# Building a four-layer network's constants earlier in the lead-in: VectorE's order of work in the first ten quarters

## The chip, the core and the metric

The kernel runs on one NeuronCore of a Trainium2 chip. The metric is the device time of one execution in microseconds (us). The profile is of one execution of the same program on the chip. The engines are TensorE (PE in the profile, PEld for its weight loads), VectorE (DVE), ScalarE (ACT), GpSimd (POOL) and the queue that issues most of the transfers (SP). Each engine takes its own instructions in program order, and semaphores tie the engines together.

## The reference, cut to what matters

The input is x of 8192 samples of 8 x 16 x 16 in float32. Four layers follow, each a residual one over a normalised input:

```
x = x + L0_conv_ref(gn(x), core0, core1, core2, bias)   # three-core tensor-train product
x = x + L1_conv_ref(gn(x), lin_w, lin_b, gamma, beta)   # 3x3 convolution, batch norm over all samples, relu
x = x + L2_conv_ref(gn(x), weight, bias)                # 3x3 convolution of quantised x and weights
x = x + L3_conv_ref(gn(x), weight, bias)                # 3x3 convolution of binarised weights, edge padding
```

`gn` is a group norm with 4 groups of 2 channels. The batch norm of layer 1 and the maximum of layer 2 need all samples, so the kernel passes over the data three times. Only the start of the first pass (layer 0 and the convolution of layer 1) matters here.

## The kernel before

**Tiles and quarters.** The samples are cut in 64 tiles of 128 samples. A tile is 128 partitions (channel and row) by 2048 elements (sample and column). Each tile is cut in four quarters of 32 samples. The first pass is the loop of lines 569 to 628 over n = 0 to 255; n is called a quarter number here, and quarter n belongs to tile t = n // 4. In quarter n, TensorE runs the second half of layer 0 for quarter n (`main`, 16 matmuls into a PSUM tile `po`), between its halves the first half of layer 0 for quarter n + 1 (`expand`, into `pu`, which ScalarE copies to `u`), and at the end, from quarter 6 on, layer 1's convolution for quarter n - 6 (`conv1`, into `pm` and `pc`). VectorE closes quarter n with `x += po` (line 414, "DVE xs<-po,xs" in the profile). The instructions of a quarter are put in order by hand: `at(r, ok, f, ...)` hangs a function on step r of the eight steps of `main`, so a lower r means an earlier place in every engine's queue.

**The norms.** Tile t + 2 is normalised for layer 0 in the quarters of tile t: its square on ScalarE (second quarter), its sums on VectorE (`norm_b_sums`, third quarter), a small chain `norm_b_stats` that ends in a power on GpSimd, and `norm_b_apply` on VectorE (fourth quarter). Tile t - 1 gets its second norm, for layer 1, in a like manner (`norm_sums`, `norm_stats`, `norm_apply`, first and second quarter). `conv1_output` on VectorE puts layer 1's output together one quarter after its matmuls.

**The halves.** From the second tile on, `expand` takes its input as two parts, a rounded high half and the rest, both read back from DRAM. `limbs(t, q)` makes them: a ScalarE copy into `xh`, a GpSimd subtraction in place ("POOL bs<-bs,xh"), and eight transfers by SP into `limb_d` ("limb_d<-xh" and "limb_d<-bs"). `fetch(t, q)` reads them back with a transfer that GpSimd issues ("xl<-limb_d"). Which quarter's halves are made where is written out in lines 614 to 617: in quarter n > 2 those of quarter n + 4, and before that by a table. GpSimd also adds layer 0's bias to each tile (`add_bias`, "POOL xs<-xs,w").

**The constants.** VectorE builds the constants of layers 1 to 3 in the lead-in, in the generator `late_constants` (lines 135 to 246). Each `next(rest, None)` at the top of a quarter issues one part, up to the next `yield`, ahead of everything else that VectorE does in that quarter. The parts are "limbs" (`core2r`), "layer 1" (group sums, `band1`, and the six combined weights `fast1`), "layer 2" (`avg16`, the quantised weights), "band 2", "layer 3" (the signs and scales), "band 3" (with `sign3`) and "statistics" (`wsum`, `quarter`, `gpad`, selectors). The condition on line 582 leaves out quarter 0 and the fourth quarter of each tile.

**Buffers.** `po`, `pm` and `pc` share three PSUM buffers in turn, so once `conv1` runs, `po` of a quarter waits for VectorE's `x += po` of the quarter before it, and `pm` and `pc` wait until `conv1_output` has read the ones before them. `pu` has one buffer, so `expand` waits for ScalarE's copy of the last one.

Of the kernel before, what the change touches and what calls it, by code (L numbers as in the profile page):

```python
# [24 lines left out]
NQ = 4  # L25
# [28 lines left out]
def tile_net(ctx: ExitStack, tc: tile.TileContext, xb, xt_in, pack0, pack1, pack2, out):  # L54
    nc = tc.nc
    NT = xt_in.shape[0]
# [33 lines left out]
    def load2(i):  # L90
        T2[i]["x"] = x_slots[i % KEEP]
        T2[i]["y"] = y_stay[i] if i < STAY else y_slots[(i - STAY + 1) % len(y_slots)]
        if i >= STAY:
            nc.sync.dma_start(T2[i]["y"], y_d[order2[i]])
            nc.sync.dma_start(T2[i]["x"], x1_d[order2[i]])
# [198 lines left out]
    with first as s:  # L294
# [19 lines left out]
        def load_b(t):  # L314
            T[t]["xb"] = bs[t % 2]
            n = F // 2 if t == 0 else F
            for a in range(0, F, n):
                nc.sync.dma_start(T[t]["xb"][:, a:a + n], xb[t][:, a:a + n])
# [84 lines left out]
        def main(t, q, between, n0=None):  # L403
            u = T[t].pop(("u", q)).rearrange("p b (s n) -> p b s n", s=R)
            po = ps_m.tile([P, BANK], F32, name=f"po_{t}_{q}", tag="mm")
            parts = [(0, QS)] if n0 is None else [(0, n0), (n0, QS)]
            for a, b in parts:
                for r in range(R):
                    for f, args in between.get(r, ()) if b == QS else ():
                        f(*args)  # L410
                    pe.matmul(samples(po)[:, a:b], core01[:, r], u[:, a:b, r, :], start=(r == 0), stop=(r == R - 1))
            cols = slice(q * BANK, (q + 1) * BANK)
            x = T[t]["x"]
            dve.tensor_tensor(x[:, cols], po, x[:, cols], ALU.add)
# [66 lines left out]
        def conv1(t, q):  # L481
            v = T[t].pop(("v", q))
            pm, po = (ps_m.tile([P, k, NC], F32, name=f"{n}_{t}_{q}", tag="mm") for n, k in (("pm", 4), ("pc", 2)))
            for ps, at in ((pm, 0), (po, 4)):
                for k in range(ps.shape[1]):
                    pe.matmul(ps[:, k], L["fast1"][:, at + k], v[:, at + k], start=True, stop=True)
            m = wk.tile([P, 2, NC], F32, name=f"m_{t}_{q}", tag="m")
            act.activation(m[:, 0], pm[:, 0], AF.Identity, bias=L["b1"], scale=1.0)
            act.copy(m[:, 1], pm[:, 2])
            T[t]["m", q] = m, pm, po  # L490
# [40 lines left out]
        def quarter_of(n, lag):  # L531

            t, q = divmod(n - lag, NQ)
            return (t, q) if 0 <= t < NT else None
# [7 lines left out]
        rest = late_constants(s.enter_context(tc.tile_pool(name="late", bufs=1)))  # L542
# [26 lines left out]
        for n in range(NT * NQ):  # L569
            t, q = divmod(n, NQ)  # L570
            steps = {}

            def at(r, ok, f, *args):
                if ok:
                    steps.setdefault(r, []).append((f, args))

            def at1(r, f, lag):
                if quarter_of(n, lag):
                    at(r, True, f, *quarter_of(n, lag))

            last, before, ahead = t == NT - 1, t > 0, t + 2 < NT
            if n > 0 and q != NQ - 1:
                next(rest, None)
            tn, qn = divmod(n + 1, NQ)
            at(0, tn < NT, expand, tn, qn, 0)
            at(4, tn < NT, expand, tn, qn, 1)
            at1(0, conv1_input, LAG)
            if n < NT * NQ - 1:
                at1(6, conv1_scaled, LAG - 1)
            if n == 0 and NT > 1:  # L590
                at(1, True, norm_b_spread, 1)
                at(1, True, norm_b_apply, 1)
                at(1, True, add_bias, 1)
            if q == 0:
                if before and t - 1 not in y_of:
                    nc.sync.dma_start(x1_d[t - 1], T[t - 1]["x"])
                at(1, before, norm_sums, t - 1)
                at(4, before, norm_stats, t - 1)
                if ahead:
                    load_b(t + 2)  # L600
            elif q == 1:
                at(1, ahead, norm_b_square, t + 2)
                at(1, before, norm_apply, t - 1)
                at(4, t + 3 < NT, load_t, t + 3)
            elif q == 2:
                at(1, ahead, norm_b_sums, t + 2)
                at(1, ahead, norm_b_stats, t + 2)
            else:
                at(1, t + 3 < NT, add_bias, t + 3)
                at(1, ahead, norm_b_spread, t + 2)  # L610
                at(1, ahead, norm_b_apply, t + 2)
            at1(3, conv1_output, LAG + 1)

            for m in {0: [], 1: [4, 5], 2: [6]}.get(n, [n + NQ]):
                at(0 if n == 1 else 2, m < NT * NQ, limbs, *divmod(m, NQ))
            for m in {0: [], 1: [4, 5], 2: []}.get(n, [n + 3]):
                at(5, m < NT * NQ, fetch, *divmod(m, NQ))
            if n == 1:
                at(5, NT > 2, add_bias, 2)
            if last:  # L620
                at(2, q > 1, quarter_apply, t, q - 2)
                at(2, q > 0, quarter_stats, t, q - 1)
            main(t, q, steps, n0=QS // 2 if n == 0 else None)
            if quarter_of(n, LAG):
                conv1(*quarter_of(n, LAG))
            if n == NT * NQ - 2 and NT > STAY + 2:
                load2(STAY)
                load2(STAY + 1)
# [435 lines left out]
```

## Time and profile before

| | |
|---|---|
| time, median of 3 | 3863.89 us (3861.8 to 3866.22) |
| span of the profiled execution | 3863.6 us |
| TensorE busy | 3612.7 us (94%) |
| VectorE busy | 3415.1 us (88%) |
| ScalarE busy | 2512.1 us (65%) |
| GpSimd busy | 3044.1 us (79%) |
| TensorE busy from 0 to 150 us | 117.14 of 150 us |
| TensorE busy from 150 to 2500 us | all but 0.04 of 2350 us |

An engine that is busy nearly all of a stretch may bound it; an idle engine with a named releaser tells what it waited for. The page's shares are averages over three passes with different limits, so a change in the lead-in is read from the timeline of the first 155 us. In a timeline line the columns are start and duration in us, engine, line, operation, output and inputs, shapes, the number of instructions merged, and in brackets the idle time before it and what ended that. Most instructions are issued through one helper and carry its line (L43), so they are told apart by the names of their tiles.

### The profile page before, as it was taken

What the parts mean: (1) busy time and instruction counts of PE and PEld (TensorE: products, weight loads), DVE (VectorE), ACT (ScalarE), POOL (GpSimd) and SP (SyncE); (2) the same over time, 40 slices, a digit from 0 to 9 for tenths busy, and PEclk for the clock granted to TensorE, in tenths of its full rate; (3) what the DMA queues carried; (4) which work ended last, traced back from release to release, by engine and by line L of the source; (5) the groups of instructions that cost most, each with busy time, mean ns of one, the idle gap of its engine ahead of it and who ended that gap; (6) DMA issues with size and microseconds to landing.
All of it is one profiled execution on the core that took longest, in us unless ns stands there. A gap on an engine that the chain in (4) does not pass through costs nothing.

```text
span 3863.6 us, 52760 instructions
## 1 busy us (share of the span) xinstructions
PE 3612.7 (94%) x16264; PEld 2130.7 (55%) x16326; DVE 3415.1 (88%) x6316; ACT 2512.1 (65%) x2673; POOL 3044.1 (79%) x3101
## 2 busy tenths in 40 slices
PE   7899999999999999999999999997665589999998
PEld 4566666666666666666666666662221145555555
DVE  7988888888888888888888888877998889999997
ACT  4566666666666666666666666665665477777775
POOL 4687777877778777777777777766887679999998
PEclk9999999999999999999999999997776699999999
DMA  5678788787887878878788788757999624444432
GB/s 210 207 253 270 253 265 266 250 269 254 264 269 249 271 252 263 269 251 268 253 264 268 253 265 255 257 185 285 423 425 425 280 92 181 185 184 183 178 153 98
DMA packets 210809, 960.93 MB, mean 249 GB/s; under 512 B 44896, under 2 KB 45152, under 8 KB 110048
## 3 DMA queue, kind: packets, MB, share of 16 engines
q1 hardware_dynamic: 173808, 692.22, 48.2%
q0 software_dynamic: 36288, 264.26, 23.2%
q8 instruction: 131, 2.15, 0.2%
q14 instruction: 150, 1.23, 0.1%
q10 hardware_dynamic: 432, 1.08, 0.1%
HBM read 578.84 MB, written 378.54 MB: 248 GB/s over the span
## 4 chain that ended last, share of the span: by engine, by line
PE 83%; DMA 6%; DVE 6%; issue 2%; POOL 1%; ACT 0%; POOLq 0%; SPq 0%; DVEq 0%; ACTq 0%
PE po L43 44%; PE pu L43 12%; PE pf L43 10%; PE pm L43 6%; PE pq L43 4%; PE s L43 3%; PE pc L43 3%; DVE top L43 2%; DMA yk<-y_d 2%; DMA x_d<-xs 1%; DMA x_d<-u 1%; DMA x_d<-xk 1%; DMA x_d<-ys 1%; DMA xk<-x_d 1%; DMA xs<-x_d 1%
## 5 line engine op out<-in xcount | busy, mean ns | idle before, releaser
L43 PE MATMUL po<-u,core 128*128 128x512 f32 (+1 forms) x4112 | 1847.0, 592 | 4.8 <-DVE xs L43 4.8
L43 ACT COPY u<-pu 128x2048 f32<-128x2048 f32 x512 | 956.4, 1868 | 527.8 <-PE pu L43 527.7
L43 PEld LDWEIGHTS po<-u,core 128*128 128x128 f32 x4112 | 745.4, 190 | 743.6 <-issue 737.5
L43 PE MATMUL pu<-core2r,xl 128*128 128x256 f32 x4032 | 679.3, 311 | 6.1 <-DMA xl<-limb_d 6.1
L43 PEld LDWEIGHTS pu<-core2r,xl 128*128 128x128 f32 x4032 | 528.8, 189 | 129.3 <-issue 128.4
L43 POOL TENSOR_TENSOR bs<-bs,xh 128x512 fp32r<-128x512 f32 (+1 forms) x253 | 324.7, 1284 | 196.0 <-ACT xh L43 196.0
L43 POOL TENSOR_TENSOR v<-e 128x128 f32<-128x128 f32 x750 | 397.4, 541 | 0.0
L43 DVE TENSOR_TENSOR xs<-po,xs 128x512 f32<-128x512 f32 x256 | 177.0, 692 | 227.1 <-PE po L43 227.1
L43 ACT ACTIVATE m<-pm,b 128x128 f32<-128x128 f32 x250 | 91.9, 368 | 405.1 <-PE pm L43 405.1
L43 PEld LDWEIGHTS pm<-v,fast 128*128 128x128 f32 x2000 | 263.7, 192 | 128.6 <-issue 109.7
L43 POOL TENSOR_TENSOR e<-x1n,x 128x512 f32<-128x512 f32 x250 | 305.9, 1224 | 23.7 <-ACT x L43 16.4
L43 DVE TENSOR_TENSOR bs<-bs,stat 128x1024 f32<-128x1024 f32 x252 | 290.8, 1216 | 2.1
L43 POOL TENSOR_TENSOR xs<-xs,w 128x2048 f32<-128x2048 f32 x64 | 291.5, 4555 | 0.5 <-DMA xs<-in_xt 0.5
L43 PE MATMUL pm<-v,fast 128*128 128x128 f32 x2000 | 265.3, 276 | 8.3 <-DVE ends L43 8.3
L43 POOL TENSOR_TENSOR mv<-mv,mhalf 128x4 f32<-128x4 f32 x127 | 130.8, 1030 | 150.3 <-DVE mv L43 150.3
L43 ACT ACTIVATE x<-x1n 128x512 f32<-128x512 f32 x500 | 246.9, 544 | 2.1 <-DVE x1n L43 2.1
L43 PE MATMUL pf<-hi,sign 128*128 128x512 f32 x768 | 226.8, 433 | 0.0
L43 POOL DMA_DIRECT2D xl<-limb_d x252 | 149.8, 594 | 97.2 <-ACT x L43 34.3
L43 PE MATMUL pf<-lo,sign 128*128 128x512 f32 x768 | 219.4, 423 | 3.4 <-ACT lo L43 3.4
L43 POOL TENSOR_TENSOR v<-r 128x128 f32<-128x128 f32 x500 | 215.5, 447 | 0.0
L43 ACT ACTIVATE sq<-xs 128x2048 f32<-128x2048 f32 (+1 forms) x107 | 199.3, 1862 | 8.0 <-POOL xs L43 4.6
L43 POOL TENSOR_TENSOR mvb<-mvb,mhalf 128x4 f32<-128x4 f32 x64 | 66.3, 1036 | 173.8 <-DVE mvb L43 173.8
(289 smaller groups left out, 7184.8 us busy)
## 6 DMA issues: line engine op xcount, KB each, us to landing
xl<-limb_d POOLq DMA_DIRECT2D x252, 1024.0 KB, 7.4
x_d<-xs SPq DMA_DIRECT2D x76, 1024.0 KB, 8.4
xs<-in_xt SPq DMA_DIRECT2D x64, 1024.0 KB, 7.5
bs<-in_xb SPq DMA_DIRECT2D x63, 1024.0 KB, 5.6
limb_d<-xh SPq DMA_DIRECT2D x1008, 64.0 KB, 4.4
limb_d<-bs SPq DMA_DIRECT2D x1008, 64.0 KB, 5.2
y_d<-ys SPq DMA_DIRECT2D x60, 1024.0 KB, 8.1
u<-x_d SPq DMA_DIRECT2D x36, 1024.0 KB, 6.1
```

What stands on the lines that cost most here:

```text
L43: return self.tc.keep_in_program_order(op(*args, **kwargs))
```

## The change

It has two parts, both in the lead-in. First, the generator is advanced in every quarter from 1 on, and twice in quarter 1. So "limbs" and "layer 1" are both built in quarter 1 (before: quarters 1 and 2), "layer 2" in quarter 2 (before 4), "band 2" in 3 (before 5), "layer 3" in 4 (before 6), "band 3" in 5 (before 8) and "statistics" in 6 (before 9). Second, the halves of quarter 7, the last of the second tile, are made in quarter 2 beside those of quarter 6, at step 0, instead of in quarter 3 at step 2; there they stood behind the third tile's `norm_b_apply` and `add_bias` in program order. Its purpose is to use VectorE's idle time in quarter 1 and to have the second tile's halves in DRAM sooner.

```diff
@@ -579,8 +579,10 @@
             last, before, ahead = t == NT - 1, t > 0, t + 2 < NT
-            if n > 0 and q != NQ - 1:
+            if n > 0:
                 next(rest, None)
+                if n == 1:
+                    next(rest, None)
             tn, qn = divmod(n + 1, NQ)
@@ -611,8 +613,8 @@
-            for m in {0: [], 1: [4, 5], 2: [6]}.get(n, [n + NQ]):
-                at(0 if n == 1 else 2, m < NT * NQ, limbs, *divmod(m, NQ))
+            for m in {0: [], 1: [4, 5], 2: [6, 7], 3: []}.get(n, [n + NQ]):
+                at(0 if n < 3 else 2, m < NT * NQ, limbs, *divmod(m, NQ))
```

## The prediction

> **What bounds the kernel now.** I began with the table of stretches, to see where TensorE is not busy.
>
> ```profile
> core 0: us, PE busy (x) PEld busy (x) DVE busy (x) ACT busy (x) POOL busy (x), PEclk, DMA share, GB/s
> 0.00:150.00 150.00, 117.14 (x495) 70.13 (x496) 127.39 (x204) 71.24 (x63) 74.21 (x86) 0.93 0.57 197
> 150.00:700.00 550.00, 550.00 (x2401) 341.18 (x2400) 487.45 (x947) 357.00 (x408) 424.78 (x583) 1.00 0.80 259
> ```
>
> From 150 us on TensorE is the bound for the rest of the first pass, at 10.08 us a quarter (the chain shows quarters ending at 154.98, 165.07, 175.14). So whatever the lead-in saves moves all that follows by the same amount, and nothing else of the change can pay. The second view is TensorE's waits from 60 to 155 us (total us, times, longest).
>
> ```profile
> PE pm L43 <- DVE ends L43: 8.3, 2, 4.2
> PE pu L43 <- DMA xl<-limb_d: 6.1, 1, 6.1
> PE po L43 <- DVE xs L43: 4.8, 2, 2.7
> ```
>
> One wait is for quarter 6's halves from DRAM, the other four for VectorE. The third view is the timeline: why is VectorE late?
>
> ```profile
> 42.08 0.69 DVE L43 TENSOR_TENSOR xs<-po,xs 128x512 f32<-128x512 f32 x1 [7.43 <-PE po L43]
> 48.57 5.07 DVE L43 TENSOR_SCALAR fast<-fast 128x128 f32<-128x128 f32 x1
> 48.95 4.59 POOL L43 TENSOR_TENSOR xs<-xs,w 128x2048 f32<-128x2048 f32 x1
> 62.01 4.55 POOL L43 TENSOR_TENSOR xs<-xs,w 128x2048 f32<-128x2048 f32 x1
> 67.74 0.62 POOL L43 DMA_DIRECT2D xl<-limb_d  x1
> 75.04 2.04 PE L43 MATMUL pu<-core2r,xl 128*128 128x256 f32 x8 [6.10 <-DMA xl<-limb_d]
> 109.59 5.13 DVE L43 TENSOR_TENSOR ys<-w,she 128x384 f32<-128x384 f32 x2
> 116.94 2.83 DVE L43 CAST sign<-band 128x384 fp32r<-128x384 f32 x1
> 130.02 5.82 DVE L43 TENSOR_SCALAR quarter<-quarter 128x4 f32<-128x4 f32 x1
> ```
>
> VectorE idles 7.43 us in quarter 1 and then is nearly gapless to 155 us. And some tiny constants take 3 to 6 us: 128x128 TENSOR_SCALARs of the same group take 0.23, and this one 5.07, ending at 53.64, just when GpSimd's `add_bias` (48.95 to 53.54) ends. Likewise `quarter`, four elements, waits from 130.02 to 135.84 while GpSimd runs without a gap to 135.81.
>
> [...]`quarter` waited out a run of nine GpSimd instructions. I use the trace: a contending instruction waits for the end of GpSimd's gapless run. [...]Here the 8 `po` matmuls after the 6.10 us wait take 4.38 us instead of 3.60, and those after a 2.71 us wait 5.12. So a removed wait also saves up to 1.5 us of slow matmuls.
>
> **The change, part by part.** The work is the same; only places move. Parts, from start to start of their neighbours: "layer 1" 42.68 to 53.83, 11.15 us, of which 4.84 is the stall shown, so 6.3 net; "layer 2" 4.4 (two short stalls of 1 us on GpSimd's subtractions; 2.4 net); "band 2" 77.34 to 80.05, 2.7; "layer 3" 86.28 to 92.93, 6.65 (4.2 stalled, 2.45 net); "band 3" 109.59 to 119.69, 10.1 (3.0 net); "statistics" 129.12 to 136.50, 7.4 (1.75 net). I place them again, taking GpSimd's and the transfers' times from the trace.
>
> *Quarter 1.* "Layer 1" starts at 34.64, when "limbs" ends. Its third tensor_tensor (36.4) meets the subtractions of 36.29 to 38.80, a stall of 2.4; it ends at 34.64 + 6.3 + 2.4 = 43.4. Behind it waits `x += po` of quarter 1, at 43.4 instead of 42.08: 1.3 us that TensorE doesn't feel, since it needs that buffer again only at 61. End 44.0.
>
> *Quarter 2.* "Layer 2" meets an idle GpSimd: 46.5. `norm_b_sums` 4.6: 51.1. The small statistics reach their tensor_scalar at 51.7, inside `add_bias` (48.95 to 53.5), behind which GpSimd now has two subtractions of 1.26 ready, quarter 6's and, moved here, quarter 7's: a run until 56.06. That is the wait the change adds, up to 4.4 us; behind it stand the power, `x += po` and all of the third tile's norm. Power 56.7 to 57.7 (before 59.76 to 60.79), `x += po` of quarter 2 by 57.3 (before 59.60). The subtractions end at 54.8 and 56.1 (before 62.0 and 67.8), so quarter 6's halves leave SP at about 55 instead of 62.07.
>
> *Quarter 3.* "Band 2" [...]stands from 57.3 against the power and the `add_bias` right behind it, 57.7 to 62.25: it can lose 4.9. Then 62.3 + 2.7 = 65.0, spread and apply 0.36 + 4.55 = 69.9, `x += po` 70.5 (before 66.4). The fetch goes out at 62.3 instead of 67.74 and, at the 7.2 us of before, lands by 69.6. But ScalarE now waits for `x += po` with its square (1.9), then the high half and the copy of `pu` (1.9 and 0.5): the one `pu` buffer is free at 74.7. So TensorE starts quarter 5 at 74.7, not 75.04: this early gain is lost again. I take this end; without the loss of 4.9 it starts at 70.
>
> *Quarters 4 and 5.* "Layer 3" 2.45: 73.0. Sums 2.3 + 2.3, statistics 1.4: 79.1 (before 76.73); quarter 7's fetch goes at 80.1 and lands at 87.7, some 2 us after TensorE wants it. `x += po` 79.7, "band 3" against a power and one subtraction, 3.0 + 1.9: 84.6; apply 5.4: 90.0; `x += po` 90.6 (before 86.3).
>
> *Quarter 6.* "Statistics" meets layer 1's input work on GpSimd (to about 92.8): 94.6. Sums 4.6, statistics 1.15, `x += po` 100.3 to 101.0 (before 98.71 to 99.4). TensorE's quarter 7 waits for that, and ends 9.35 later as before: 110.4, against 108.96. Up to here I am 1.4 us behind, but every constant is built.
>
> *Quarters 7 to 10.* No "band 3", no "statistics": 10.1 + 7.4 = 17.5 us of VectorE are gone. Quarter 8: 111.1 + 2.3 (sums) + 2.8 (conv1_output) + 3.7 (sums, statistics) = 119.9, `x += po` 120.6 (before 128.48 to 129.2). TensorE runs quarter 8 to 121.0 with no wait (its pm starts there, before 123.22), quarter 9 to 131.1 (before 139), convolution to 132.4 without the wait until 143.05, quarter 10 to 141.2. Before, this was 154.82. VectorE has 131.8 + 4.6 + 1.15 + 2.8 = 140.4 and is in time. **Gain 154.8 - 141.2 = 13.6 us**, so 3863.9 - 13.6 = 3850.3.
>
> Check from the other side: with no wait at all after 68.93, TensorE takes 2 x 8.75 (quarters 5 and 6) and 4 x 10.08 and would be at 126.8, so 28 is the ceiling.
>
> **The rivals.**
> (A) The stalls shift only, as worked out: 3850. [...]Chance 0.50.
> (B) "Band 2" slips in ahead of `add_bias`, or waits little: 4.9 us less in the whole chain, and some of "statistics" (2): 13.6 + 4.9 + 2 = 20, 3844. For: between subtractions and power GpSimd has a gap. Chance 0.23.
> (C) VectorE loses more than I placed. GpSimd's runs grow when both are late: "layer 3" and "band 3" could each lose another 4 as "layer 3" does before. Gain 13.6 - 8 = 5.6: 3858, within or near 0.2%. Chance 0.20.
> (D) Slower. The constants ahead of the third and fourth tile's norms delay fetches, the delays reach TensorE in quarters 5 to 7[...], and the freed quarters 8 to 10 are refilled by them: three long stalls like `quarter`'s 5.8 above (C) and one slow restart, 17.4 + 1.5 - 5.6 = 13.3 us lost: 3877. Against: before holds 23 us of such stalls already, and filling the idle 7.4 us is work taken off. Chance 0.07.
>
> **How the numbers follow.** The forecast is A, 3850.3. The range covers A with B's end (3844, less 2 for the spread of runs[...]) and C's (3858 and 2): 3841 to 3860; D and the tails are left out. Faster by over 0.2% (below 3856.2): A, B and a fifth of C, 0.77; within: the rest of C, 0.16; slower 0.07.
>
> **What would show it.** Right: the idle before `x += po` of quarter 1 gone; "layer 1" with a stall of about 2.4; tensor_scalar of the third tile's statistics stalled to about 56; the fetch of quarter 6 near 62; a long "band 2" tensor_tensor beside `add_bias`; `po` of quarter 7 near 101; no TensorE waits for VectorE in quarters 8 to 10; convolution of quarter 10 near 141; and from there 10.08 a quarter. Wrong: a TensorE wait in quarters 8 to 10, a start of quarter 5 after 76 or near 70, or a gain that is not kept at 2500 us.

## The result, and the profile after

| | before | after |
|---|---|---|
| time, median | 3864.78 us (3861.8 to 3867.38, 6 runs) | 3848.18 us (3845.82 to 3849.26, 6 runs) |
| ratio, 95% interval | | 0.9956 [0.9943, 0.9969] |
| span of the profiled execution | 3863.6 us | 3844.7 us |
| TensorE busy from 0 to 150 us | 117.14 us | 129.84 us |

The change makes the kernel 16.6 us faster in this series; the interval is 12 to 22 us. 13.6 were forecast. The two profiled executions differ by more, 18.9 us of span: before's took 0.6 us more than its median, after's 1.7 less. Before's own executions spread widely: in the later series its median lay between 3861.1 and 3862.3 and single ones between 3855 and 3869, while the changed kernel's six stayed within 3.5 us; the last experiments ask why.

The first view is the table of stretches after the change, with the same columns as in the prediction.

```profile
0.00:150.00 150.00, 129.84 (x582) 78.10 (x583) 134.34 (x242) 82.01 (x77) 91.11 (x108) 0.95 0.65 221
150.00:700.00 550.00, 550.00 (x2397) 340.86 (x2396) 488.03 (x943) 359.04 (x410) 421.94 (x585) 1.00 0.80 262
```

From 150 us on TensorE is busy throughout, as before; the gain lies in the first row. TensorE's waits from 60 to 155 us were 19.2 us in five pieces (8.3 + 6.1 + 4.8); now they are 6.6 in three:

```profile
PE pu L43 <- ACT u L43: 4.6, 1, 4.6
PE po L43 <- DVE xs L43: 1.7, 1, 1.7
PE pu L43 <- DMA xl<-limb_d: 0.3, 1, 0.3
```

That is 12.6 us of waiting less, and TensorE's busy time up to 150 us grew by 12.7. But quarter 10's convolution starts 18.5 us sooner, counted from the same matmuls of quarter 1 (below). The other 5.9 us are, by subtraction, matmuls that ran slow after the waits of before, where eight of `po` take 3.60 us when nothing holds them up:

```profile
99.45 5.12 PE L43 MATMUL po<-u,core 128*128 128x512 f32 x8 [2.71 <-DVE xs L43]
123.22 2.05 PE L43 MATMUL pm<-v,fast 128*128 128x128 f32 x8 [4.20 <-DVE ends L43]
129.22 5.40 PE L43 MATMUL po<-u,core 128*128 128x512 f32 x8 [2.05 <-DVE xs L43]
```

After the change eight matmuls of `pm` take 1.05 us in every quarter, and only quarter 5 restarts slowly (4.81 us for the eight of `po`).

The third view is the timeline after, VectorE and GpSimd together. The whole trace of after is 0.93 us early against before's (the same eight `po` matmuls of quarter 1 start at 32.70 and 33.63); the comparisons below add that.

```profile
35.39 1.66 DVE L43 TENSOR_TENSOR ys<-ys 128x384 f32<-128x384 f32 x1
...
41.99 0.68 DVE L43 TENSOR_TENSOR xs<-po,xs 128x512 f32<-128x512 f32 x1
...
47.79 4.61 POOL L43 TENSOR_TENSOR xs<-xs,w 128x2048 f32<-128x2048 f32 x1
...
50.34 4.53 DVE L43 TENSOR_SCALAR mvb<-mvb 128x8 f32<-128x8 f32 x1
...
52.30 2.54 POOL L43 TENSOR_TENSOR bs<-bs,xh 128x512 fp32r<-128x512 f32 x2
...
56.37 4.84 POOL L43 TENSOR_TENSOR xs<-xs,w 128x2048 f32<-128x2048 f32 x1
...
56.84 4.78 DVE L43 TENSOR_TENSOR ys<-ys 128x384 f32<-128x384 f32 x1
...
72.60 2.08 PE L43 MATMUL pu<-core2r,xl 128*128 128x256 f32 x8 [4.59 <-ACT u L43]
...
96.61 3.70 PE L43 MATMUL po<-u,core 128*128 128x512 f32 x8 [1.72 <-DVE xs L43]
```

The 7.43 us idle before `x += po` of quarter 1 is gone: its line has no bracket any more. The two waits of VectorE that the change was forecast to add are there: the tensor_scalar of the third tile's statistics ends at 54.87, with GpSimd's run of add_bias and two subtractions (54.84), and a tensor_tensor of "band 2" stands beside the next add_bias. And the large stalls of before, 5.07 in "layer 1", 4.36 in "layer 3" (the line below), 4.39 (of the 5.13) and 2.83 in "band 3" and 5.82 in "statistics", have no counterpart of that size in the same parts: after 62 us no constant takes over 1.6 us. From quarter 8 on TensorE waits for VectorE no more.

```profile
87.26 4.36 DVE L43 TENSOR_SCALAR mean<-mean 128x8 f32<-128x8 f32 x1
```

### The profile page after: what moved, and what is told of

The parts are those of the page before. It is cut to its first block, busy times and chain, and to the rows that moved or that the text cites. A ratio compares the mean times of both kernels' runs of the same rounds, so it can differ in the third digit from the quotient of the medians.

```text
span 3844.7 us, 52821 instructions
## 1 busy us (share of the span) xinstructions
PE 3612.3 (94%) x16326; PEld 2127.7 (55%) x16326; DVE 3402.9 (89%) x6316; ACT 2511.3 (65%) x2673; POOL 3043.5 (79%) x3101
## 4 chain that ended last, share of the span: by engine, by line
PE 84%; DVE 7%; DMA 6%; issue 1%; POOL 1%; ACT 0%; POOLq 0%; DVEq 0%; SPq 0%
PE po L43 44%; PE pu L43 12%; PE pf L43 10%; PE pm L43 6%; PE pq L43 4%; PE s L43 3%; PE pc L43 3%; DVE top L43 2%; DMA yk<-y_d 1%; DMA x_d<-xk 1%; DMA x_d<-xs 1%; DMA xk<-x_d 1%; DMA xs<-x_d 1%; DVE ys L43 1%; POOL xs L43 0%
## 5 line engine op out<-in xcount | busy, mean ns | idle before, releaser
L43 PE MATMUL pq<-q,band 128*128 128x480 bf16 (+1 forms) x768 | 192.2, 388 | 6.8 <-ACT q L43 3.9
```

The source lines that it names most:

```text
L43: return self.tc.keep_in_program_order(op(*args, **kwargs))
```

## The experiments

The theory was the prediction's: VectorE bounds quarters 2 to 10, and what pays is its work moved into idle time and its stalls on GpSimd. The rivals: the halves that reach DRAM sooner carry the gain, or only the filled idle time does. Beside each median stands the record's ratio to before in the same series. It is not the plain quotient of the two medians; where the two tell different gains, both are given. A lead-in is counted in a trace from quarter 1's first `po` matmul to the start of quarter 10's convolution: 121.2 us in before, 102.7 in after.

**Constants alone.** The generator's calls as in the change, the halves' table as before; the edit is shown against the changed kernel.

```diff
-            for m in {0: [], 1: [4, 5], 2: [6, 7], 3: []}.get(n, [n + NQ]):
-                at(0 if n < 3 else 2, m < NT * NQ, limbs, *divmod(m, NQ))
+            for m in {0: [], 1: [4, 5], 2: [6]}.get(n, [n + NQ]):
+                at(0 if n == 1 else 2, m < NT * NQ, limbs, *divmod(m, NQ))
```

> The constants as in the changed kernel, the halves of quarters 6 and 7 where they were before. Theory (VectorE bounds quarters 2 to 10; the gain is its work moved into idle time and stalls on GpSimd avoided): nearly the whole gain stays, 14 to 19 us below before. The tensor_scalar of the third tile's statistics then waits for add_bias alone and ends some 2.5 us sooner than in the changed kernel (near 52.4 in its trace, not 54.8), while the fetch of quarter 6 goes out about as late as in the changed kernel (61 to 62). Rival (the gain is the halves that reach DRAM sooner, 6.1 us of transfer wait and what it drags along): at most half, under 9 us.

Measured: 3848.97 us, ratio 0.9959 [0.9947, 0.9972], against 0.9956 for the whole change. The ratio is 15.8 us of gain, inside the 14 to 19 expected; the median is 12.8 below before's in that series, just outside. The lead-in is 102.4 us. Its timeline has the statistics' wait halved:

```profile
51.92 2.09 DVE L43 TENSOR_SCALAR mvb<-mvb 128x8 f32<-128x8 f32 x1
```

That trace is 1.56 us late against after's, so the end, 54.01, is 52.45 in after's time, as expected, and the fetch of quarter 6 at 63.39 is 61.8. The constants carry the whole gain, as far as these intervals can tell. The moved halves lengthen the statistics' wait by 2.4 us and bring nothing that shows in the time.

**Halves alone.** Only the two lines of the halves' table changed, against before.

```diff
-            for m in {0: [], 1: [4, 5], 2: [6]}.get(n, [n + NQ]):
-                at(0 if n == 1 else 2, m < NT * NQ, limbs, *divmod(m, NQ))
+            for m in {0: [], 1: [4, 5], 2: [6, 7], 3: []}.get(n, [n + NQ]):
+                at(0 if n < 3 else 2, m < NT * NQ, limbs, *divmod(m, NQ))
```

> The halves of quarter 7 in quarter 2 as in the changed kernel, the constants where they were before. Theory: the fetch of quarter 6 goes out about 2.4 us sooner (65.4 instead of 67.7), TensorE starts quarter 5 that much sooner, and it is lost again at quarter 7, where TensorE waits for VectorE: 0 to 2 us below before. Rival (the halves carry the gain): 6 us or more below.

Measured: 3861.65 us, ratio 0.9996 [0.9989, 1.0002]: nothing that is clear of the spread, as the theory had it, and the first rival is out. But the fetch did not go out 2.4 us sooner; it went at 67.86. Layer 1's last tensor_scalar now stood behind add_bias and both subtractions:

```profile
48.78 7.44 DVE L43 TENSOR_SCALAR fast<-fast 128x128 f32<-128x128 f32 x1
```

That is 2.4 us more than the 5.07 of before, and the power behind it came 2.4 us later. The fetch, with no subtraction in front of it any more, came when it came in before. The halves that were ready sooner paid for themselves with the run that they lengthened. (One trace is not the median: this one's lead-in is 117.9 us, 3.3 shorter than before's; but from the first pass's last convolutions to the end it took 1241.7 us, before's 1238.7.)

**Layer 1's constants alone in quarter 1.** Against before.

```diff
-            if n > 0 and q != NQ - 1:
+            if n == 1 or n > 2 and q != NQ - 1:
                 next(rest, None)
+                if n == 1:
+                    next(rest, None)
```

> Layer 1's constants in quarter 1, all other constants and the halves where they were before. Theory: VectorE gains the 6.3 us of work moved into idle time, less what the third tile's statistics lose behind add_bias, and the later stalls of layer 3, band 3 and statistics (4.2, 7 and 5.6 us in before) stay of that order: 6 to 10 us below before, clearly less than the changed kernel. Rival (only the filled idle time counts, the other constants' places do not matter): the same as the changed kernel, 15 to 19 below.

Measured: 3859.18 us, ratio 0.9988 [0.9982, 0.9995]: 2.6 us by the medians, 4.6 by the ratio, 1.9 to 7.0 by its interval. Both expectations missed, the rival's by far more. Filling the idle time alone brings a small part of the gain. The trace shows what keeps the rest away:

```profile
49.10 4.60 DVE L43 TENSOR_SCALAR mvb<-mvb 128x8 f32<-128x8 f32 x1
80.83 4.77 DVE L43 TENSOR_SCALAR own<-own 128x8 f32<-128x8 f32 x1
101.82 6.18 DVE L43 TENSOR_TENSOR ys<-w,she 128x384 f32<-128x384 f32 x2
120.98 5.84 DVE L43 TENSOR_SCALAR quarter<-quarter 128x4 f32<-128x4 f32 x1
```

VectorE arrives sooner and meets GpSimd all the same: a new stall in the statistics of the third tile, and the old ones of "layer 3", "band 3" and "statistics" in their old places. The profiled execution was this kernel's fastest, 3855.72, and its lead-in is 111.7 us, 9.5 shorter than before's: as much as the theory had. Why the other executions gained less is not shown.

**One part in every quarter, but no second one in quarter 1.** Against before.

```diff
-            if n > 0 and q != NQ - 1:
+            if n > 0:
                 next(rest, None)
```

> One part of the constants in every quarter from 1 on (no second one in quarter 1), so layer 1 stays in quarter 2 and the idle time of quarter 1 stays; the halves where they were before. Theory: VectorE's work up to quarter 10 is unchanged, so only avoided stalls pay: 3 to 10 us below before. Rival (only the filled idle time counts): no change, within 2 us.

Measured: 3869.24 us, ratio 1.0013 [1.0004, 1.0021]: slower, by 5.0 us (7.5 by the medians). Both missed. The trace has the clearest line of the study; some of GpSimd's instructions stand below it.

```profile
105.07 12.19 DVE L43 COPY gpad<-quarter 128x16 f32<-128x16 f32 x1
...
105.47 1.22 POOL L43 TENSOR_TENSOR e<-x1n,x 128x512 f32<-128x512 f32 x1
...
109.73 4.50 POOL L43 TENSOR_TENSOR xs<-xs,w 128x2048 f32<-128x2048 f32 x1
...
116.00 1.22 POOL L43 TENSOR_TENSOR e<-x1n,x 128x512 f32<-128x512 f32 x1
117.17 0.47 POOL L43 TENSOR_TENSOR r<-x 128x128 f32<-128x128 f32 x1
```

A copy of 16 elements a partition stood from 105.07 to 117.26, through some dozen GpSimd instructions, and ended 0.09 us into one of 0.47. TensorE waited 13.68 us for VectorE behind it. ("Layer 1", in quarter 2 as in before, had its stall as well: 5.00 us.)

**The same with the last part's copies on ScalarE.** "Statistics" makes six copies; here ScalarE does them, and multiplications by 1.0 (one in "layer 3", one in "statistics") are left out. Against the kernel just above.

```diff
-        dve.tensor_copy(wsum[:, 0, 0:G], grp)
+        act.copy(wsum[:, 0, 0:G], grp)
...
-        dve.tensor_copy(gpad[:, :, 0:G], quarter.unsqueeze(1).to_broadcast([P, NQ, G]))
+        act.copy(gpad[:, :, 0:G], quarter.unsqueeze(1).to_broadcast([P, NQ, G]))
...
```

> The kernel with one part of the constants in every quarter (it took 3869.24 us, and in its trace a copy of 128x16 elements took 12.19 us while GpSimd ran without a gap), with the six copies of its last part, statistics, on ScalarE, and the multiplications by 1.0 left out. Theory[...]: the 12.19 us and the 2.60 us copy behind it are gone, TensorE's 13.68 us wait for VectorE shrinks to under 4 us, and the time falls by 8 to 13 us, to 3856 to 3861, below the kernel before. Rival (the copy waited for data or for a transfer, which would hold ScalarE's copies as well): within 3 us of 3869.

Measured: 3849.03 us, ratio 0.9967 [0.9955, 0.998], 20 us below the kernel that it was made from (in another series). The stall is gone and TensorE's long wait with it; the longest for VectorE is

```profile
PE po L43 <- DVE xs L43: 2.2, 1, 2.2
```

The rival is out: the copy had waited for no data. But 20 us is 7 more than the most expected, and the trace shows a second cause, so the copies alone may be worth less. The last tensor_scalar of "layer 1", still in quarter 2, went by just ahead of GpSimd:

```profile
48.65 0.23 DVE L43 TENSOR_SCALAR fast<-fast 128x128 f32<-128x128 f32 x1
48.95 0.59 POOL L43 DMA_DIRECT2D xl<-limb_d  x1 [6.18 <-DMA limb_d<-xh]
```

In before the fetch came at 48.39 and the tensor_scalar at 48.57, and took 5.07. Here it came 0.30 us ahead of the fetch, there 0.18 behind it: half a microsecond decides over 4.8.

**The fourth tile's add_bias out of "band 2"'s way.** It stood at quarter 3, step 1. This and the next two are edits of the changed kernel, which was not run again in their series.

```diff
-                at(1, t + 3 < NT, add_bias, t + 3)
+                at(1, t > 0 and t + 3 < NT, add_bias, t + 3)
...
+            if n == 5:
+                at(6, NT > 3, add_bias, 3)
```

> The changed kernel with the fourth tile's add_bias moved from quarter 3, step 1, to quarter 5, step 6. In the changed kernel band 2 stood 4.8 us behind it and TensorE then waited 4.6 us at quarter 5 for ScalarE, which had waited for VectorE. Theory[...]: band 2's tensor_tensor falls from 4.78 to under 1.5, the fetch of quarter 6 goes out some 3 us sooner (58 instead of 61.2), the wait at quarter 5 shrinks to under 2 us, and some 1 to 4 us of it reach the end, unless add_bias stalls statistics in its new place: 3844 to 3848. Rival (transfers[...] set the start of quarter 5): the wait stays at 4 us or more and the time does not change.

Measured: 3849.07 us, ratio 0.9967 [0.9954, 0.9979], no better than the change and outside the 3844 to 3848 expected; the lead-in is 105.0 us, 2.3 longer than after's. Every first step came: "band 2" ran at 0.56 us an instruction, the fetch went out at 58.23, the wait at quarter 5 was 0.37. Then "band 3", earlier as well, met the moved add_bias:

```profile
75.17 6.95 DVE L43 TENSOR_TENSOR ys<-ys 128x384 f32<-128x384 f32 x1
...
75.32 1.28 POOL L43 TENSOR_TENSOR bs<-bs,xh 128x512 fp32r<-128x512 f32 x1
76.54 0.60 POOL L43 DMA_DIRECT2D xl<-limb_d  x1
77.13 4.56 POOL L43 TENSOR_TENSOR xs<-xs,w 128x2048 f32<-128x2048 f32 x1
```

**Both out of the way.** The third tile's add_bias as well, from quarter 1 to quarter 3, step 6.

```diff
-            if n == 1:
-                at(5, NT > 2, add_bias, 2)
+            if n == 3:
+                at(6, NT > 2, add_bias, 2)
+            if n == 5:
+                at(6, NT > 3, add_bias, 3)
```

> The changed kernel with the third tile's add_bias moved from quarter 1 to quarter 3, step 6, and the fourth tile's to quarter 5, step 6. Theory: the tensor_scalar of the third tile's statistics, 4.53 us in the changed kernel, and band 2's tensor_tensor, 4.78, both fall under 1 us; a stall of about 1 to 2 us comes to layer 3 and of about 2 to 4 us to statistics instead; TensorE starts quarter 5 with at most 1 us of waiting and quarter 10's convolution is 4 to 7 us sooner than in the changed kernel: 3841 to 3845. Rival (VectorE's own work, not the stalls, fills quarters 2 to 7): within 2 us of the changed kernel.

Measured: 3843.67 us, ratio 0.9955 [0.9941, 0.9969]. As the theory had it: the statistics' tensor_scalar takes 0.40 us, "band 2" shows no stall, TensorE starts quarter 5 without a wait, and the smaller stalls foreseen came instead, 1.5 us on three copies of "layer 3" and some 2 in "statistics". TensorE's one wait left is 3.0 us at quarter 7. The lead-in is 132.29 - 34.36 = 97.9 us, against 135.37 - 32.70 = 102.7 in after. The ratios to before do not tell this kernel from the change (0.9955 and 0.9956); that it is better rests on the trace and on the kernels' own times, 3843.0 to 3845.1 against 3845.8 to 3849.3, from two series.

**Both, and the copies of "statistics" on ScalarE.** The last two edits on ScalarE and on add_bias together, on the changed kernel.

```diff
-                at(1, t + 3 < NT, add_bias, t + 3)
+                at(1, t > 0 and t + 3 < NT, add_bias, t + 3)
...
-            if n == 1:
-                at(5, NT > 2, add_bias, 2)
+            if n == 3:
+                at(6, NT > 2, add_bias, 2)
+            if n == 5:
+                at(6, NT > 3, add_bias, 3)
...
-        dve.tensor_copy(wsum[:, 0, 0:G], grp)
+        act.copy(wsum[:, 0, 0:G], grp)
...
```

> The changed kernel with both add_bias moved as in the kernel above (third tile's to quarter 3, fourth tile's to quarter 5) and the copies of statistics on ScalarE. Theory: with the stalls of quarters 2, 3 and 6 gone TensorE waits under 2 us in all from quarter 4 on and quarter 10's convolution is 6 to 9 us sooner than in the changed kernel, close to the TensorE bound: 3838 to 3842. Rival (what is left of the lead-in is TensorE's and the transfers'): within 2 us of the changed kernel.

Measured: 3840.24 us, ratio 0.9948 [0.9936, 0.9961], 20.9 us below before in that series, as expected: the lowest median of all (one of its five executions took 3847.05). TensorE's waits from 60 to 165 us are one line,

```profile
PE pu L43 <- ACT u L43: 1.3, 1, 1.3
```

and the lead-in is 127.85 - 33.30 = 94.6 us, 8.1 less than after's. Most of what the change had left was thus stalls on GpSimd: moving add_bias, which takes no work from VectorE, brought 4.7 of the 8.1 us.

**The race in before.** The kernel before with the third tile's add_bias behind the power of its statistics (quarter 2, step 1), and a second trace of before itself.

```diff
                 at(1, ahead, norm_b_stats, t + 2)
+                if n == 2:
+                    at(1, True, add_bias, 2)
...
             if n == 1:
-                at(5, NT > 2, add_bias, 2)
```

> The kernel before with the third tile's add_bias moved from quarter 1, step 5, to quarter 2, step 1, behind the power of the third tile's statistics; constants and halves as before. In before the last tensor_scalar of layer 1 starts at 48.57, between the fetch at 48.39 and that add_bias at 48.95, and stands 4.84 us behind it; in the run with the copies of statistics on ScalarE the same instruction went by 0.3 us ahead of the fetch and took 0.23. Theory[...]: with add_bias gone from there the instruction always takes about 0.23, the single times lie within 5 us of each other, and the median is 3 to 7 us below before's. Rival (before's spread comes from elsewhere, such as the transfers of the later passes): the same spread of some 10 us or more, and less than 2 us gained.

> The kernel before, unchanged, for a second trace. Theory: if this execution takes under 3862, layer 1's last tensor_scalar took about 0.23 in it; if over 3864, about 5. Rival: its duration has nothing to do with the time.

Measured: 3864.75 us (3861.02 to 3868.0, 13 runs), ratio 1.0006 [0.9997, 1.0014]; and 3861.41 for the second trace, in which layer 1's last tensor_scalar, as expected for a time under 3862, went by in front of the fetch:

```profile
48.49 0.23 DVE L43 TENSOR_SCALAR fast<-fast 128x128 f32<-128x128 f32 x1
49.66 0.59 POOL L43 DMA_DIRECT2D xl<-limb_d  x1 [7.05 <-DMA limb_d<-xh]
```

and the first pass reached its last convolutions 4.3 us sooner after quarter 1's `po` (2620.46 - 33.54 against 2624.87 - 33.63). So the race, which of the two engines comes first, is in before, in these two traces. The moved add_bias missed its expectation: layer 1's instruction took 0.23 us as foreseen, but the run of GpSimd moved to 55.26 to 66.8, and "layer 2" stood there instead:

```profile
61.10 4.50 DVE L43 TENSOR_SCALAR avg_b<-avg_b 128x8 f32<-128x8 f32 x1
```

Its executions still spread over 7.0 us (before's over 9.1 in that series). So the race may add to before's spread, but how much of it is not shown; a part arises behind the first pass, as the 3 us between two traces above show.

## Why the prediction was right, point by point

**The bound and the path.** Right. The first pass is TensorE's from 150 us on, and the gain is carried through: quarter 10's convolution is 154.82 - 135.37 = 19.5 us sooner (18.5 without the traces' shift), the last convolutions of the pass 19.8 and the end of the span 18.9 (both with the shift).

```profile
154.82 1.05 PE L43 MATMUL pm<-v,fast 128*128 128x128 f32 x8
135.37 1.05 PE L43 MATMUL pm<-v,fast 128*128 128x128 f32 x8
```

**Quarters 1 to 3.** Right to about 1.3 us. "Layer 1" was to stall 2.4 us on two subtractions; its two longer tensor_tensors took 1.66 and 1.51 instead of 0.56 each, together 2.05. The statistics' stall was put at up to 4.4 and took 4.53 in place of 0.17; "band 2" was put at 4.9 and took 4.78 in place of 0.56. That these would stall was the author's estimate; before's trace has stalls on both kinds, 5.07 us on a tensor_scalar in place of 0.23 and 5.13 on two tensor_tensors that took 1.01 in after. TensorE starts quarter 5 at 73.5 in before's time (forecast 74.7), held by ScalarE's copy of `pu`, as worked out.

**The size.** Too small by 4.9 us in the trace, in two terms. In quarters 4 to 6 I had "band 3" at 4.9 us and "statistics" at 4.0; they took 4.06 (77.32 to 81.38) and 2.80 (87.29 to 90.09). With the 1.3 us from quarter 3 that is 3.3, and `x += po` of quarter 6 was done at 97.5 in before's time, not 101.0: 3.5 us. For "statistics" the prediction's rule failed, taken from the stall of `quarter` in before, that such an instruction waits for the end of GpSimd's gapless run: its first two copies were done at 88.34, within a run that ended at 89.41 (last section). And quarter 7 was to take TensorE 9.35 us "as before", with slow matmuls after the wait. It waited only 1.72 and its eight matmuls took 3.70 us, not 5.12; the quarter took 7.91: 1.4 us. The term for slow matmuls was carried over from a wait of 2.71 us and did not hold for the shorter one. From there the forecast had 30.8 us to quarter 10's convolution and it took 30.85. That is partly luck: three quarters of 10.08 are 30.24, the forecast gives no reason for its other half microsecond, and the trace spent as much, 0.29 of it on a fetch.

So the picture of the stalls was right, and the result of 3848.2, between A's 3850 and B's 3844, is A's picture with smaller stalls late in it.

**The rivals.** B's picture, "band 2" in ahead of add_bias, did not come. C's, longer stalls in "layer 3" and "band 3", did not either: "layer 3" had none. D, slower by long stalls, did not come for this change, but the kernel without the second part in quarter 1 went that way: 12.19 us on one copy, and 1.0013.

**The halves.** Their move was costed at a longer wait of the statistics against an earlier fetch, with the early gain lost again. The two single-part kernels agree: with the constants alone 0.9959, with the halves alone 0.9996. The edit of the table does one thing more than the text on the change says: it brings quarter 6's halves from step 2 to step 0 of quarter 2 too, ahead of the third tile's power. That is why two subtractions stand right behind add_bias; with the constants alone quarter 6's came at 55.50, after the power at 54.48.

## What to carry to other kernels

Count VectorE's small instructions by what GpSimd has queued when they arrive, not by their size: `quarter`, four elements, took 5.82 us in before, to the end of GpSimd's run, and 0.58 in after. Moving such work paid where it met no more of GpSimd than a fetch (in quarter 1 of after layer 1's last tensor_scalar took 0.24 us, in quarter 2 of before 5.07), and elsewhere moved the stall, as in several of these kernels (6.95 us on "band 3", 4.50 on "layer 2"). Giving the copies to ScalarE and putting `add_bias` beside work that it did not lengthen (`norm_b_apply` took 4.61 us there, and 4.61 in after with GpSimd idle) took 8.1 us more from the lead-in. A stall that half a microsecond decided is no fixed cost (5.07 us in one trace of before, 0.23 in the other): take a second trace. And a wait of TensorE can cost more than its length: 5.9 of the 18.5 us that the lead-in gained were, by subtraction, matmuls that no longer ran slow after one.

## What of the hardware was not expected

A small instruction of VectorE waited not for one instruction of GpSimd but through several: 12.19 us for a 128x16 copy (0.17 in before) past some dozen GpSimd instructions, none longer than 4.5 us. But it isn't always the whole run either: "statistics" in after ran beside layer 1's input work on GpSimd (85.10 to 89.41) with no stall over 0.7 us:

```profile
87.44 0.90 DVE L43 COPY wsum<-grp 128x4 f32<-128x4 f32 x2
87.86 0.86 POOL L43 TENSOR_TENSOR v<-r 128x128 f32<-128x128 f32 x2
88.86 0.58 DVE L43 TENSOR_SCALAR quarter<-quarter 128x4 f32<-128x4 f32 x1
```

Some of VectorE's work showed no such wait: in after two reductions into `sumb` took 2.33 us beside `add_bias` (47.31 to 49.64; it began at 47.79), and the two before them 2.34 with GpSimd idle to 47.24. What decides at which of GpSimd's instructions a wait ends, and which of VectorE's instructions wait, stays open.

TensorE's granted clock was 0.72 from 69 to 75 us in before and 0.65 from 75 to 80, in and after the wait of 6.10 us, and 1.00 from 60 to 69 and from 80 to 90. How long a wait TensorE stands without a slow restart is no sharp line here. At the start of quarter 7 the eight `po` matmuls took 3.70 us after waits of 1.10, 1.69, 1.72 and 1.95 us, and 5.1 to 5.4 after 2.31, 2.53, 2.71 and 3.00. After 2.22 us they took 5.40 in one kernel (the copies on ScalarE), and after 2.23 us 3.70 in another (before with the moved add_bias).
